# Running counts in PSUM, half a block at a time, and one PSUM bank for ranks and sums

## The chip, the cores and the metric

The kernel runs on one core of a Trainium2 chip. The metric is the device time of one execution in microseconds (us), lower is better. A core has a matrix engine (TensorE, PE in the profile; its weight loads are PEld), a vector engine (VectorE, DVE), a scalar engine (ScalarE, ACT), a general engine (GpSimd, POOL) and a queue engine that mostly issues transfers (SyncE, SP). Each works through its own instructions in order. They share an on-chip memory, SBUF, and an accumulator memory, PSUM, of eight banks with 512 fp32 values per partition each, into which TensorE writes.

## The reference

One layer of a graph network on 12,500 nodes with 64 features and 212,500 edges that are sorted by `dst`; `src` is in no order.

```python
h = jnp.maximum(_layernorm(x), 0.0)
edge_in = jnp.concatenate([h[src], h[dst], dist], axis=1)
e = silu(edge_in @ eW1 + eb1)
e = silu(e @ eW2 + eb2)
agg = jax.ops.segment_sum(e, src, num_segments=12500)
node_in = jnp.concatenate([h, agg], axis=1)
out = x + silu(node_in @ nW1 + nb1) @ nW2 + nb2
```

The sum over the edges goes by `src`, so edges that are far apart in the list are added to one node.

## The kernel before

**Buckets.** The nodes lie in 100 buckets of 125 (bucket = `src` mod 100). The edges are cut into 208 blocks of 1,024 (`BLK`), and the blocks into 11 chunks: the first has 8 blocks, the others 20 (the last of all is a little short). The work on a chunk has two halves.

- *Sending* (`count`, `send`): for each block, the share of every edge that comes from `dst` and the edge's weight is computed, and each edge's row is written to a place of its own in a DRAM table `q` of the chunk, in the part of its bucket.
- *Steps* (the `s_...` functions): the rows are fetched bucket by bucket, the share of `src` is added, both layers are applied and the rows of a bucket are summed per node. A step is four tiles of 128 rows. A batch is four buckets: one step in the first chunk, two in the others. There are 525 steps.

While the steps of chunk c run, chunk c+1 is sent. A fetch of a chunk's rows (`fetch`, issued on SP) can start when all scatters into its table are done.

**Where in its bucket does an edge go?** `count(s)` answers this for block s on DVE. `oh` (100 x 1,024, line 303) is 1 where an edge belongs to a bucket. A scan over the 1,024 columns (line 306) makes the running count `run` of each bucket: at each column it adds `oh` and a second input, `nil`, that is zero everywhere, and it starts from the last column of the block before (`carry`) or from -1. `nil` is one column, read with a stride of zero. The product of `run` and `oh` (line 314) is `own`, which keeps for each edge only the count of its own bucket. In `send(s)` eight matmuls against a column of fours (line 333) sum `own` over the buckets into `rank`, 128 x 8, and one DVE instruction (line 353) makes the row numbers `to` from it. Then POOL issues eight indirect transfers (line 362, "scatters"), each of 128 rows that are read at `qs` in SBUF and written to `q` at the rows in `to`.

**Where things lie.** All eight PSUM banks are taken: four for the rotating buffers tagged `mm`, two for `p2`, and two in the pool `sg`: one for `misc` (two rank buffers of 8 columns, used in turn by even and odd blocks, and the zero `nil`) and one for `seg`, the sums of a batch, 128 x 4 x 125. `oh`, `run` and `own` lie in SBUF (`own` twice).

**Order.** The order on PE, DVE, ACT and SP is the order of the program text; semaphores are put in from what each instruction reads and writes. A step's turn is the list at line 515: pt of the next step, the add of an earlier one's sums (`s_add`, which reads `seg` into `aggT`, once a batch), oneT, a hook, the bias, p2, one, a hook, `s_seg` (the matmuls into `seg`, line 497), a hook, lr, a hook. At the hooks the pieces of sending are put in at an even pace. A block has three pieces, and each goes one part on in `count(s + 1)` and then one part in `send(s)`:

1. pick and oh (lines 302, 303); the rank matmuls;
2. the load of edge weights and the scan; the matmuls qp with their copies on ACT, `to`, and the first four scatters;
3. the product own; the other four scatters.

`qs` has eight buffers of half a block and `to` four of a block, so POOL can be up to four blocks behind before ACT and DVE wait for it.

Of the kernel before, what the change touches and what calls it, by code (L numbers as in the profile page):

```python
# [38 lines left out]
P = 128  # L39
L = 125  # L40
# [19 lines left out]
def tile_gnn(ctx: ExitStack, tc: tile.TileContext, x, src, dst, ew, eW1, eb1, eW2, eb2, nW1, nb1, nW2, nb2, out):  # L60
# [178 lines left out]
    with ExitStack() as work:  # L239
# [5 lines left out]
                engines={mybir.EngineType.PE, mybir.EngineType.DVE, mybir.EngineType.Activation, mybir.EngineType.SP}  # L245
            )
        )
        misc = sgp.tile([P, 4 * TB], F32, name="misc")
        nc.vector.memset(misc[:, 2 * TB : 2 * TB + 1], 0.0)
        nil = misc[:NB, 2 * TB : 2 * TB + 1]  # L250
        oh = cnt.tile([NB, BLK], F16, name="oh")
        run = cnt.tile([NB, BLK], F32, name="run")
        carry = {}
        blk = {}
        nblocks = -(-E // BLK)
# [40 lines left out]
        def count(s):  # L296

            if s >= nblocks:
                return
            c = chunk_of[s]  # L300
            bc, bb, win, pick = blk[s]
            nc.vector.tensor_scalar(pick, bc, same, plus, op0=OP.is_equal, op1=OP.add)
            nc.vector.tensor_scalar(oh, bb[:NB, :], part[:NB, :], None, op0=OP.is_equal)
            yield
            weights(s)
            nc.vector.tensor_tensor_scan(  # L306
                run, oh, nil.to_broadcast([NB, BLK]), carry.get(c, -1.0), op0=OP.add, op1=OP.add
            )
            yield
            n = min(BLK, E - s * BLK)  # L310
            end = run[:, n - 1 : n]
            carry[c] = end
            own = wk.tile([NB, BLK], F16, name="own")
            nc.vector.tensor_tensor(own, run, oh, op=OP.mult)  # L314
            blk[s].append(own)
            if s + 1 == nblocks or chunk_of[s + 1] != c:
                u = wk.tile([NB, 1], F32, name="u")
                for limit, op in ((chunks[c][2] * P - 1, OP.is_gt), (chunks[c][3] - 1, OP.is_lt)):
                    nc.vector.tensor_scalar(u, end, float(limit), None, op0=op)
                    nc.vector.tensor_tensor(bad[:NB, 1:2], bad[:NB, 1:2], u, op=OP.add)  # L320
            yield

        def send(s):

            p, g = s // 2, s % 2
            c = chunk_of[s]
            _, _, cap, _, q = chunks[c]
            _, _, win, pick, run = blk.pop(s)
            n = min(BLK, E - s * BLK)
            nt = -(-n // P)  # L330
            rank = misc[:, (s % 2) * TB : (s % 2 + 1) * TB]
            for t in range(nt):
                nc.tensor.matmul(rank[:, t : t + 1], run[:, t * P : (t + 1) * P], fours[:NB, :], start=True, stop=True)  # L333
            yield

            qps = [mm.tile([P, G, H], F32, name="qp", tag="mm") for _ in range(2)]
            for t in range(G):
                for a in range(2):
                    half = slice(a * HB, a * HB + WL + 2)
                    if a * G + t < nt:  # L340
                        nc.tensor.matmul(  # L341
                            qps[a][:, t, :], pick[half, t * P : (t + 1) * P], win[half, :], start=True, stop=True
                        )
            halves = []
            for t0 in range(0, nt, G):
                qs = qsp.tile([P, G, W], F32, name="qs")
                m = min(G, nt - t0)
                nc.scalar.copy(qs[:, :m, :H], qps[t0 // G][:, :m, :])  # L348
                halves.append((t0, m, qs))
            for t0, m, qs in halves:  # L350
                if t0 == 0:
                    to = top.tile([P, TB], I32, name="to")
                    nc.vector.scalar_tensor_tensor(
                        to[:, :nt], rank[:, :nt], float(G * cap * P), bkE[:, g * TB : g * TB + nt, p], op0=OP.min, op1=OP.add
                    )
                at = g * TB + t0
                nc.scalar.copy(
                    qs[:, :m, H:], locE[:, at : at + m, p][:, :, None].to_broadcast([P, m, W - H])
                )
                for t in range(t0, t0 + m):  # L360
                    k = min(P, n - t * P)
                    i = nc.gpsimd.indirect_dma_start(  # L362
                        out=q[:],
                        out_offset=bass.IndirectOffsetOnAxis(ap=to[:k, t : t + 1], axis=0),
                        in_=qs[:k, t - t0, :],
                        in_offset=None,
                    )

                    tc.declare_no_dep(i.ins, group=f"rows{c}", reason="each edge has a row of its own")
                    tc.add_to_no_dep_group(f"rows{c}", i.ins)  # L370
                yield
# [25 lines left out]
        def fetch(i):  # L397
            if i >= len(batches):
                return
            c, B, n = batches[i]  # L400
            assert pending[c] == 0
            while B not in done_a:
                next(feed)
            q = chunks[c][-1]
            at = B * G * n * P
            qt = ld2.tile([P, G * most, W], F32, name="qt")
            nc.sync.dma_start(
                qt[:, : G * n, :].rearrange("p j w -> p (j w)"),
                q[at : at + G * n * P, :].rearrange("(p j) w -> p (j w)", p=P),
            )  # L410
            a3 = ld2.tile([P, G, 3, H], BF16, name="a3")
            nc.sync.dma_start(
                a3.rearrange("l b s f -> l b (s f)"), ta_buckets[:, B * G : B * G + G]
            )
            batch[c, B] = [qt, a3, None]
            if c == len(chunks) - 1:
                node_in[B] = nodes_in(B, ndp[0])

# [3 lines left out]
            return batch[c, B], [((g * G + t) % n * G + (g * G + t) // n, (g * G + t) // n) for t in range(G)]  # L422

        def s_lr(k):
            (qt, _, _), tiles = of(k)
            loc = qt.rearrange("p j w -> p (j w)").bitcast(BF16)
            lr = mm.tile([P, G, P], F32, name="lr", tag="mm")
            for t, (j, _) in enumerate(tiles):
                at = 2 * (j * W + H) + 1
                nc.tensor.matmul(lr[:L, t, :], loc[:, at : at + 1].to_broadcast([P, L]), identb, start=True, stop=True)  # L430
            st[k] = {"lr": lr}
# [5 lines left out]

        def s_pt(k):

            (qt, a3, _), tiles = of(k)  # L440
            oneT = st[k].pop("oneT")
            pt = mm.tile([P, G, P], F32, name="pt", tag="mm")
            for t, (j, _) in enumerate(tiles):
                nc.tensor.matmul(  # L444
                    pt[:, t, :], qt[:, j, :H], ident, is_transpose=True, start=t == 0, stop=False, skip_group_check=True
                )
            for b, same in itertools.groupby(range(G), lambda t: tiles[t][1]):
                same = list(same)
                cols = slice(same[0], same[-1] + 1)
                for i in range(3):  # L450
                    nc.tensor.matmul(  # L451
                        pt[:, cols, :], a3[:L, b, i, :], oneT[:, cols, :], start=False, stop=i == 2, skip_group_check=True
                    )
            e1 = wk.tile([P, G, P], F32, name="e1")
            nc.scalar.activation(e1, pt, AF.Silu)  # L455
            st[k]["e1"] = e1

        def s_one(k):
            (qt, _, _), tiles = of(k)
            c, B, n, g = steps[k]  # L460
            wide = [P, G // n, n, L]
            loc = qt[:, : G * n, H : H + 1].rearrange("p (j b) w -> p b j w", b=G)
            one = wk.tile([P, G, L], F32, name="one")
            nc.vector.tensor_tensor(  # L464
                one.rearrange("p (b j) l -> p b j l", j=n),
                nodes1[:, None, None, :].to_broadcast(wide),
                loc[:, tiles[0][1] : tiles[0][1] + G // n].to_broadcast(wide),
                op=OP.is_equal,
            )
            st[k]["one"] = one  # L470
            if g == n - 1:
                fetch(c * (NB // G) + B + NQ)
# [16 lines left out]

        def s_seg(k):  # L490
            c, B, n, g = steps[k]
            item, tiles = of(k)
            if g == 0:
                item[2] = sgp.tile([P, G, L], F32, name="seg")
            e2, one = st[k].pop("e2"), st[k].pop("one")
            for t, (j, b) in enumerate(tiles):
                nc.tensor.matmul(item[2][:, b, :], e2[:, t, :], one[:, t, :], start=j < G, stop=j >= G * (n - 1))  # L497

        def s_add(k):
            c, B, n, g = steps[k]  # L500
            if g < n - 1:
                return
            v = aggT[:, B * G : B * G + G, :]
            seg = batch.pop((c, B))[2]
            if c == 0:
                nc.vector.tensor_copy(v, seg)  # L506
            else:
# [425 lines left out]
```

## Time and profile before

| | |
|---|---|
| time, median of 3 runs | 2703.32 us (2700.62 to 2704.18) |
| the profiled execution | 2702.45 us |
| its span, first to last instruction | 2700.7 us |
| PE busy | 2188.2 us (81%) |
| DVE busy | 1874.6 us (69%) |
| POOL busy | 1818.5 us (67%) |
| ACT busy | 1251.1 us (46%) |
| mean TensorE clock granted | 0.907 |

The profile is of one execution. A group of instructions is named by its line in the kernel, its engine and operation, and what it writes and reads; behind it stand the count, the busy time, the mean duration of one in ns, and the idle time of the engine in front of it with what ended it. "Issue" is time in which the engine waited for nothing that the profile shows. The timeline lists instructions in order: start in us, duration in us, engine, line, operation; in brackets the idle time ahead of it. The windows view gives each engine's busy time and instruction count within stretches of the span. The chain of work that ended last puts 63% of the span on PE, 13% on DMA, 6% on issue, 5% on POOL and 2% on DVE.

### The profile page before, as it was taken

To read this page: it belongs to the slowest core of one execution; us is meant where nothing else is said; L and a number is where in the kernel's file an instruction comes from. 1 tells how busy PE (TensorE), PEld (TensorE's weight loads), DVE (VectorE), ACT (ScalarE), POOL (GpSimd) and SP (SyncE) were. 2 spreads that over 40 slices of the span, in tenths; PEclk is the share of its full clock that TensorE was granted. 3 is DMA by queue.
4 is the path that set the end of the run, shared out by engine and by line. 5 is a ranking of instruction groups with operands and counts; after the bars stand their busy time and mean duration, and the time that the engine had idled before them with its cause. 6 is when DMAs were issued, how large, how long until landed. Compare 5 with 4: busy or idle time off the path is not lost.

```text
span 2700.7 us, 59194 instructions
## 1 busy us (share of the span) xinstructions
PE 2188.2 (81%) x21814; PEld 2043.3 (76%) x21814; DVE 1874.6 (69%) x2634; ACT 1251.1 (46%) x2689; POOL 1818.5 (67%) x1728
## 2 busy tenths in 40 slices
PE   2436674898699599699879969959959987997997
PEld 1326574897699599599779869959958986996996
DVE  4736683796588488588768858848857885883443
ACT  2325551454355255355445535525535544553443
POOL 2546787777777777777777777777777777773000
PEclk9757786998899799799989989979989998998999
DMA  8668675876776777686787777767767755764441
GB/s 201 190 186 243 202 246 163 260 234 196 231 234 229 213 248 236 203 251 231 212 256 230 237 218 233 238 205 253 231 202 250 240 183 198 234 199 158 158 164 52
DMA packets 257969, 577.18 MB, mean 214 GB/s; under 512 B 51201, under 2 KB 110579, under 8 KB 257468
## 3 DMA queue, kind: packets, MB, share of 16 engines
q1 hardware_dynamic: 185096, 384.91, 44.3%
q0 software_dynamic: 54144, 123.04, 12.6%
q10 hardware_dynamic: 18434, 65.37, 10.5%
q8 instruction: 175, 2.87, 0.4%
q14 instruction: 120, 0.98, 0.1%
HBM read 361.44 MB, written 211.67 MB: 212 GB/s over the span
## 4 chain that ended last, share of the span: by engine, by line
PE 63%; DMA 13%; issue 6%; POOL 5%; DVE 2%; ACT 1%; SPq 0%; DVEq 0%; POOLq 0%; ACTq 0%
PE p L483 15%; PE seg L497 15%; PE pt L451 11%; DMA q<-qs,to 8%; PE pt L444 8%; PE qp L341 7%; POOL q L362 5%; PE lr L430 4%; DMA pick<-in_edge_weight_dram 3%; PE misc L333 1%; DMA bb<-rows 1%; PE z L216 1%; PE o L225 1%; DVE oneT L435 1%; PE z L219 1%
## 5 line engine op out<-in xcount | busy, mean ns | idle before, releaser
L362 POOL DMA_INDIRECT q<-qs,to x1661 | 1780.4, 1072 | 632.2 <-issue 445.6
L455 ACT ACTIVATE e<-pt 128x512 f32<-128x512 f32 x525 | 313.9, 598 | 778.0 <-PE pt L451 765.1
L483 PE MATMUL p<-w,e 128*128 128x128 f32 x4200 | 588.2, 284 | 2.2 <-ACT p L477 2.2
L497 PE MATMUL seg<-one,e 128*128 128x125 f32 x4200 | 576.8, 281 | 8.9 <-DVE aggT L506 5.7
L483 PEld LDWEIGHTS p<-w,e 128*128 128x128 f32 x4200 | 529.5, 198 | 27.5 <-issue 10.4
L497 PEld LDWEIGHTS seg<-one,e 128*128 128x128 f32 x4200 | 524.8, 196 | 11.2 <-ACT p L477 4.1
L435 DVE TENSOR_SCALAR oneT<-lr,part 125x512 bf16<-125x512 f32 x525 | 392.6, 748 | 197.5 <-PE lr L430 194.6
L306 DVE TENSOR_TENSOR_SCAN run<-oh,run,misc 100x1024 f32<-100x1024 f16 x197 | 461.1, 2341 | 1.0 <-PE misc L333 0.7
L451 PE MATMUL pt<-oneT,a 125*128 125x256 bf16 (+1 forms) x3300 | 444.6, 274 | 0.0
L341 PE MATMUL qp<-win,pick 50*128 50x128 f32 x3322 | 264.6, 300 | 205.0 <-DMA pick<-in_edge_weight_dram 119.9
L348 ACT COPY qs<-qp 128x512 f32<-128x512 f32 x416 | 224.7, 588 | 444.3 <-PE qp L341 312.0
L341 PEld LDWEIGHTS qp<-win,pick 50*128 50x128 f32 x3322 | 224.1, 202 | 237.8 <-issue 208.2
L444 PE MATMUL pt<-ident,qt 128*128 128x128 f32 x2100 | 332.8, 282 | 68.8 <-DVE oneT L435 68.8
L508 DVE TENSOR_TENSOR aggT<-aggT,seg 128x500 f32<-128x500 f32 x250 | 168.3, 673 | 315.7 <-PE seg L497 313.3
L464 DVE TENSOR_TENSOR one<-nodes,qt 128x500 f32<-128x500 f32 x525 | 353.4, 673 | 0.5 <-PE seg L497 0.5
L451 PEld LDWEIGHTS <-a 125*128 125x128 bf16 x3300 | 320.5, 100 | 34.5
L487 ACT ACTIVATE e<-p 128x512 f32<-128x512 f32 x525 | 314.6, 599 | 12.3 <-PE p L483 11.6
L477 ACT COPY p<-b2f 128x512 f32<-128x512 f32 x525 | 312.3, 595 | 0.1
L444 PEld LDWEIGHTS pt<-ident,qt 128*128 128x128 f32 x2100 | 228.4, 145 | 74.9 <-DVE oneT L435 72.9
L430 PE MATMUL lr<-identb,qt 128*125 128x128 bf16 x2100 | 215.1, 226 | 63.1 <-DMA qt<-q 63.0
L314 DVE TENSOR_TENSOR own<-run,oh 100x1024 f16<-100x1024 f32 x208 | 253.7, 1220 | 0.0
L430 PEld LDWEIGHTS <-qt 128*125 128x125 bf16 x2100 | 187.8, 140 | 75.6 <-DMA qt<-q 63.7
(122 smaller groups left out, 1094.5 us busy)
## 6 DMA issues: line engine op xcount, KB each, us to landing
qt<-q SPq DMA_DIRECT2D x250, 576.0 KB
a<-ta SPq DMA_DIRECT2D x275, 384.0 KB
q<-zeros ACTq DMA_DIRECT2D x30, 1638.0 KB
bb<-rows SPq DMA_DIRECT2D x208, 224.0 KB
bc<-rows SPq DMA_DIRECT2D x208, 128.0 KB
q<-qs,to POOLq DMA_INDIRECT x1661
win<-tb SPq DMA_DIRECT2D x416, 24.0 KB
ta<-parts SPq DMA_DIRECT2D x25, 384.0 KB
```

What stands on the lines that cost most here:

```text
L306: nc.vector.tensor_tensor_scan(run, oh, nil.to_broadcast([NB, BLK]), carry.get(c, -1.0), op0=OP.add, op1=OP.add)
L341: nc.tensor.matmul(qps[a][:, t, :], pick[half, t * P : (t + 1) * P], win[half, :], start=True, stop=True)
L362: i = nc.gpsimd.indirect_dma_start(out=q[:], out_offset=bass.IndirectOffsetOnAxis(ap=to[:k, t : t + 1], axis=0), in_=qs[:k, t - t0, :], in ...
L430: nc.tensor.matmul(lr[:L, t, :], loc[:, at : at + 1].to_broadcast([P, L]), identb, start=True, stop=True)
L435: nc.vector.tensor_scalar(oneT, st[k].pop("lr")[:L], part1[:L, :], None, op0=OP.is_equal)
L444: nc.tensor.matmul(pt[:, t, :], qt[:, j, :H], ident, is_transpose=True, start=t == 0, stop=False, skip_group_check=True)
L451: nc.tensor.matmul(pt[:, cols, :], a3[:L, b, i, :], oneT[:, cols, :], start=False, stop=i == 2, skip_group_check=True)
L455: nc.scalar.activation(e1, pt, AF.Silu)
L464: nc.vector.tensor_tensor(one.rearrange("p (b j) l -> p b j l", j=n), nodes1[:, None, None, :].to_broadcast(wide), loc[:, tiles[0][1] : ti ...
L483: nc.tensor.matmul(p2[:, t, :], e1[:, t, :], w2, start=False, stop=t == G - 1, skip_group_check=True)
L487: nc.scalar.activation(e2, p2, AF.Silu)
L497: nc.tensor.matmul(item[2][:, b, :], e2[:, t, :], one[:, t, :], start=j < G, stop=j >= G * (n - 1))
```

## The change

`run` becomes a PSUM tile of half a block (512 fp32 columns, one whole bank), in one buffer. The scan and the product are each done twice, for columns 0 to 511 and 512 to 1,023: scan, product, then the end of the piece, then scan and product of the second half. The second scan starts from the last column of the first; the carry from block to block is read from `run` too. So piece 2 has one half scan and one half product, and piece 3 the same; before, the scan was in piece 2 and the product in piece 3. `own` is allocated one piece earlier, ahead of the first scan.

To make room for `run` in PSUM, `misc` and `seg` become one tile in one bank: columns 0 to 499 are `seg`, columns 500 to 507 the one `rank` buffer. The sums of every batch lie in this tile for the whole run; before, a tile was allocated for each batch from a pool with one buffer. `nil` moves from PSUM to a column of its own in SBUF.

```diff
-        misc = sgp.tile([P, 4 * TB], F32, name="misc")
-        nc.vector.memset(misc[:, 2 * TB : 2 * TB + 1], 0.0)
-        nil = misc[:NB, 2 * TB : 2 * TB + 1]
+        misc = sgp.tile([P, G * L + TB], F32, name="misc")
+        seg = misc[:, : G * L].rearrange("p (b l) -> p b l", l=L)
+        rank = misc[:, G * L :]
+        run = sgp.tile([NB, HALF], F32, name="run")
         oh = cnt.tile([NB, BLK], F16, name="oh")
-        run = cnt.tile([NB, BLK], F32, name="run")
+        nil = cnt.tile([NB, 1], F32, name="nil")
+        nc.vector.memset(nil, 0.0)
...
             weights(s)
-            nc.vector.tensor_tensor_scan(
-                run, oh, nil.to_broadcast([NB, BLK]), carry.get(c, -1.0), op0=OP.add, op1=OP.add
-            )
-            yield
-            n = min(BLK, E - s * BLK)
-            end = run[:, n - 1 : n]
-            carry[c] = end
             own = wk.tile([NB, BLK], F16, name="own")
-            nc.vector.tensor_tensor(own, run, oh, op=OP.mult)
             blk[s].append(own)
+            for h in range(2):
+                half = slice(h * HALF, (h + 1) * HALF)
+                n = min(HALF, E - s * BLK - h * HALF)
+                if n <= 0:
+                    break
+                nc.vector.tensor_tensor_scan(
+                    run, oh[:, half], nil.to_broadcast([NB, HALF]), carry.get(c, -1.0), op0=OP.add, op1=OP.add
+                )
+                end = carry[c] = run[:, n - 1 : n]
+                nc.vector.tensor_tensor(own[:, half], run, oh[:, half], op=OP.mult)
+                if h == 0:
+                    yield
...
-            rank = misc[:, (s % 2) * TB : (s % 2 + 1) * TB]
...
-            if g == 0:
-                item[2] = sgp.tile([P, G, L], F32, name="seg")
             e2, one = st[k].pop("e2"), st[k].pop("one")
             for t, (j, b) in enumerate(tiles):
-                nc.tensor.matmul(item[2][:, b, :], e2[:, t, :], one[:, t, :], start=j < G, stop=j >= G * (n - 1))
+                nc.tensor.matmul(seg[:, b, :], e2[:, t, :], one[:, t, :], start=j < G, stop=j >= G * (n - 1))
...
             v = aggT[:, B * G : B * G + G, :]
-            seg = batch.pop((c, B))[2]
+            del batch[c, B]
```

More of the change, by code (lines that the diff above doesn't have):

```diff
@@ L414, in fetch @@
             )
-            batch[c, B] = [qt, a3, None]
+            batch[c, B] = [qt, a3]
             if c == len(chunks) - 1:
@@ L424, in s_lr @@
         def s_lr(k):
-            (qt, _, _), tiles = of(k)
+            (qt, _), tiles = of(k)
             loc = qt.rearrange("p j w -> p (j w)").bitcast(BF16)
@@ L438, in s_pt @@
         def s_pt(k):
-            (qt, a3, _), tiles = of(k)
+            (qt, a3), tiles = of(k)
             oneT = st[k].pop("oneT")
@@ L458, in s_one @@
         def s_one(k):
-            (qt, _, _), tiles = of(k)
+            (qt, _), tiles = of(k)
             c, B, n, g = steps[k]
@@ L491, in s_seg @@
             c, B, n, g = steps[k]
-            item, tiles = of(k)
-            if g == 0:
-                item[2] = sgp.tile([P, G, L], F32, name="seg")
+            _, tiles = of(k)
             e2, one = st[k].pop("e2"), st[k].pop("one")
             for t, (j, b) in enumerate(tiles):
-                nc.tensor.matmul(item[2][:, b, :], e2[:, t, :], one[:, t, :], start=j < G, stop=j >= G * (n - 1))
+                nc.tensor.matmul(seg[:, b, :], e2[:, t, :], one[:, t, :], start=j < G, stop=j >= G * (n - 1))
         def s_add(k):
```

## The prediction, made before the changed kernel was run

> **What bounds the kernel now.** I read the clock view first (0.907 on one core, nothing odd), then the windows by stage, cut at the ends of the chunks.
>
> ```profile
> core 0: us, PE busy (x) PEld busy (x) DVE busy (x) ACT busy (x) POOL busy (x), PEclk, DMA share, GB/s
> 240.00:460.00 220.00, 140.79 (x1380) 127.62 (x1380) 148.70 (x211) 103.96 (x238) 161.00 (x137) 0.77 0.63 203
> 680.00:901.00 221.00, 192.22 (x1979) 182.11 (x1980) 167.11 (x230) 107.09 (x230) 168.52 (x160) 0.94 0.73 230
> 1564.00:1785.00 221.00, 191.97 (x1982) 181.71 (x1981) 167.97 (x230) 107.67 (x230) 169.41 (x162) 0.93 0.73 231
> 2451.00:2701.00 250.00, 228.37 (x1951) 206.16 (x1951) 95.88 (x157) 103.30 (x204) 19.46 (x27) 0.96 0.42 139
> ```
>
> By busy time PE leads (192 of 221 us) and POOL stands at 169. But the line of the scatters says otherwise:
>
> ```profile
> L362 POOL DMA_INDIRECT q<-qs,to x1661: 889/967/3041, 67.7 to 2451.3; - x185
>   issue: 445.6, 1340
> ```
>
> A scatter takes 0.967 us, and the next one starts 0.30 us later although nothing is named that it waits for: one scatter each 1.27 us is POOL's own pace. A chunk has 20 blocks of 8 scatters. In chunk 3 (first scatter 691.9, last end 913.5, 221.6 us by the timeline) 160 x 1.27 = 203.2; scatters longer than 0.967 add 14.6, and gaps longer than 0.30 only 4.2. Chunks 3 to 9 are all so (219.7 to 221.3 us). So POOL sets the period of a chunk, and PE's 29 idle us are back-pressure: PE waits 19.15 us at 1564 for work whose loads stand in SP's queue behind a fetch that waits for the chunk's last scatter. After 2451 no scatter is left, and PE's 250 us of tail follow.
>
> The question is what stretches a scatter. I laid POOL's rows of the timeline against DVE's:
>
> ```profile
> 1564.12 2.34 DVE L306 TENSOR_TENSOR_SCAN run<-oh,run,misc 100x1024 f32<-100x1024 f16 x1
> 1564.62 0.97 POOL L362 DMA_INDIRECT q<-qs,to  x1 [0.30 <-issue]
> 1565.89 0.97 POOL L362 DMA_INDIRECT q<-qs,to  x1 [0.30 <-issue]
> 1566.37 0.14 DVE L353 SCALAR_TENSOR_TENSOR to<-misc,bkE 128x8 int32<-128x8 f32 x1
> 1566.43 0.67 DVE L464 TENSOR_TENSOR one<-nodes,qt 128x500 f32<-128x500 f32 x1
> 1567.01 1.22 DVE L314 TENSOR_TENSOR own<-run,oh 100x1024 f16<-100x1024 f32 x1
> 1567.16 1.92 POOL L362 DMA_INDIRECT q<-qs,to  x1 [0.30 <-issue]
> 1569.38 0.96 POOL L362 DMA_INDIRECT q<-qs,to  x1 [0.30 <-issue]
> ```
>
> Under the scan (inputs oh in SBUF and nil in PSUM) two scatters keep 0.97. The one that starts under own (run and oh, both in SBUF) takes 1.92 and ends 0.85 after own. Over the run, 210 scatters overlap a scan and no other DVE instruction: their mean excess is 0.001 us. 14 overlap own alone: 0.61. 44 overlap the add into aggT alone (one input in PSUM): 0.00. Instructions with a broadcast second input in SBUF stretch scatters too: beside L527 and L536 (mean and var) a scatter that starts 0.2 us in loses up to 0.67. Total excess over 0.967 is 175.6 us.
>
> [...]
>
> **The change part by part.**
>
> *Own from PSUM.* The product now has one SBUF input (oh). Of the 102.1 us of excess in chunks 3 to 9 (140 blocks, 0.73 each), 55 scatters end 0.84 behind own and carry 43.0 us, and 80 that are held by one and then by own carry 16.1; half of these to own makes 51 us, 0.36 a block. Shared out by overlap over the whole run, own has 81.4 us, 0.39 a block. I take 0.37 as what goes.
>
> *The scan with nil in SBUF.* This is the part that costs. The scan's two inputs are then oh and nil, both in SBUF, which it wasn't before, and it comes twice a block. No run shows such a scan. Bounds: nothing if the scan doesn't hold POOL; about 0.95 us a half (what a scatter lost at the worst phase of own) if each half does its worst, 1.9 a block. I take the rule that own's rows give: a scatter that starts under the instruction ends 0.84 after it, one started up to 0.5 before it ends 0.30 before its end. Applied to a 1.28 us instruction at the 140 places where scans start now, it gives 0.77 each, because starts cluster 0.15 and 0.42 us ahead of a scatter. At even phase it gives 0.68, times 0.73 (for own the rule gives 0.44 at its true places against 0.61 at even phase) 0.49. A held POOL also shifts its own phase, so I take the mean, 0.63, for the first half. The second lies where own lay: 0.39 x 1.28/1.22 = 0.40. Together 1.03 a block. Net 1.03 - 0.37 = +0.66 us a block, x 200 blocks of chunks 1 to 10 = +132 us. Chunk 0 (8 blocks) has 44 us of other gaps between its scatters; half price, +3.
>
> *DVE's time.* Rows: 500 elements 673 ns (L464), 1,024 elements 1,220 (L314), so 1.044 ns an element and 151 fixed; a PSUM input costs no more (L508, 500 elements, also 673). A half product is 686, two 1,371: +151. The scan with a constant start is 2,278, with a carried one 2,341: 2.08 ns an element, 151 fixed, 63 for the carry. A half is 1,277, two 2,554: +213. Writing PSUM instead of SBUF is not in the trace; I take it equal, within 0.1 us a half. In all +364 ns a block, 76 us of DVE time. It is hidden: DVE idles 53 us a chunk and gets 7 more. Without that cover it would be the 76 us.
>
> *Split of the pieces.* DVE's longest stretch ahead of oneT falls from 2.34 to 1.28 + 0.69 = 1.97, the next grows from 1.22 to 1.97. PE's 68.8 us of waits for oneT are mostly back-pressure (DVE stands 7.63 us at `to` for a scatter's DMA at 1554), so nothing.
>
> *Seg and rank in one bank, one rank buffer.* New waits: seg's matmuls for the `to` in front of them, rank's matmuls for the add into aggT, `to` for the seg matmuls in front. Behind a waiting seg stand lr, pt and all of PE; `to` is queued behind a half scan and a half product, at worst 1.97 us, x 20 = 39 us a chunk if nothing covers it. Cover: p2 or qp of the same turn (1.1 us each on PE) and PE's 29 idle us a chunk. DVE has run ahead to wait for seg 134 times (313 us), so `to` mostly comes early. Between 0 and 39 a chunk; I take 0, as PE's loss up to 29 only eats its wait for POOL. The memory that run frees in SBUF is used by nothing. Loads and scatters keep their number and order.
>
> *Sum.* 2702.45 (the profiled execution, 1.75 above its span, 0.9 under the median) + 132 + 3 = 2837 us.
>
> **Rivals.**
> - *The scan with a stride-0 nil does not hold POOL* (faster). Price: only own's 0.37 goes, x 200 = 74 us, so 2628; PE's 192 us still fit in 214 a chunk. For it: nil is one column, and no scan with two SBUF inputs was seen. Against it: mean and var are broadcast too and hold. It decides as soon as a half scan holds POOL for under 0.18 us.
> - *The product still holds POOL through its one SBUF input* (it doesn't do what it says). Two products of 0.69; one (0.67) lost 0.1 to 0.45 by phase when a scatter started under it. 0.15 each, +0.30 a block: 2837 + 60 = 2897. Against it: L508 reads one operand of each kind and cost nothing.
> - *The bank's waits bind PE.* If all 39 us a chunk show, 10 over PE's slack: +100, hidden in a POOL that is itself 13 us a chunk slower; on top of a faster POOL it would undo the gain, 2700.
> - *Half holding*: 0.3 a half, +0.23 a block, 2750.
>
> **How the numbers follow.** Forecast 0.66, with its own range 2770 (net 0.34 a block) to 2900 (0.98); product also holds 0.09; between, by the last two rivals, 0.07; scan doesn't hold 0.18. From 2680 to 2930 lie 0.65 of the first, 0.08 of the second and the 0.07: 0.80. This kernel's three times lie within 0.13%, so 0.2% (5.4 us) is what can be told from no change. Faster 0.20 (the 0.18 and a little of the 0.07), same 0.02, slower 0.78.
>
> **What would show it.** In the changed trace: a chunk's period near 234 us with 160 scatters; scatters beside a lone half scan with a mean excess of 0.4 or more, ending 0.84 behind it; those beside a lone half product at 0; L362's mean about 1,150 ns against 1,072; half scans near 1,277 ns and half products near 686; seg's waits for `to` small. Wrong if scatters keep 0.97 under half scans, if chunks fall to 213 us, or if PE's idle time is named by the bank's waits while POOL starves.

## The result, and the profile after

The changed kernel takes 2717.64 us (median of 9 runs, 2712.54 to 2721.56), the kernel before 2703.27 us (9 runs). The ratio is 1.0054, 95% interval 1.0041 to 1.0067: slower by 14 us, where the forecast had 134. The span of its profiled execution is 2719.8 us, 19.1 more than before.

The windows view of the changed kernel, with the windows of the prediction (busy us and count for PE, PEld, DVE, ACT and POOL, then clock, DMA share, GB/s; the last window reaches to the end):

```profile
680.00:901.00 221.00, 192.77 (x1973) 182.00 (x1974) 170.07 (x263) 106.92 (x229) 170.03 (x160) 0.93 0.70 223
1564.00:1785.00 221.00, 193.12 (x1980) 182.02 (x1980) 174.19 (x267) 106.86 (x228) 169.71 (x159) 0.93 0.73 230
2451.00:2720.00 269.00, 233.69 (x2011) 211.14 (x2009) 98.60 (x162) 106.38 (x210) 35.01 (x42) 0.94 0.40 133
```

The stages look alike; POOL still handles its 160 scatters a chunk, and its last one ends 20 us later (2472.1 against 2452.2), so the tail begins 20 us later and is as long as before. By the timeline chunks 3 to 9 take 223.5 us on average from the first scatter's start to the last one's end (before 220.9; forecast 234). The groups of instructions that the prediction priced:

```profile
L367 POOL DMA_INDIRECT q<-qs,to x1661 | 1795.4, 1081 | 637.0 <-issue 450.7
...
L315 DVE TENSOR_TENSOR_SCAN run<-oh,run,nil 100x512 f32<-100x512 f16 x405 | 523.0, 1291 | 0.1
...
L319 DVE TENSOR_TENSOR own<-run,oh 100x512 f16<-100x512 f32 x416 | 287.7, 691 | 14.2
```

A half scan takes 1,291 ns and a half product 691, as priced (1,277 and 686). But the mean scatter went from 1,072 to 1,081 ns only, not to 1,150. Does a half scan hold POOL at all (does a scatter that meets it have to wait for its end)? The timeline of the changed kernel, DVE and POOL rows side by side, two places:

```profile
843.60 0.67 DVE L469 TENSOR_TENSOR one<-nodes,qt 128x500 f32<-128x500 f32 x1
844.18 1.29 DVE L315 TENSOR_TENSOR_SCAN run<-oh,run,nil 100x512 f32<-100x512 f16 x1
844.54 1.70 POOL L367 DMA_INDIRECT q<-qs,to  x1 [0.30 <-issue]
845.51 0.69 DVE L319 TENSOR_TENSOR own<-run,oh 100x512 f16<-100x512 f32 x1
...
1603.05 0.67 DVE L469 TENSOR_TENSOR one<-nodes,qt 128x500 f32<-128x500 f32 x1
1603.37 1.18 POOL L367 DMA_INDIRECT q<-qs,to  x1 [0.30 <-issue]
1603.63 1.29 DVE L315 TENSOR_TENSOR_SCAN run<-oh,run,nil 100x512 f32<-100x512 f16 x1
1604.86 0.97 POOL L367 DMA_INDIRECT q<-qs,to  x1 [0.31 <-issue]
1604.96 0.69 DVE L319 TENSOR_TENSOR own<-run,oh 100x512 f16<-100x512 f32 x1
```

It does. The scatter that starts 0.36 us into the half scan takes 1.70 us and ends 0.77 after the scan (846.24 against 845.47). The scatter at 1603.37 starts ahead of the half scan and under `one`. It takes 1.18 us and ends 0.83 after `one` (1604.55 against 1603.72): that is the hold of `one`, and the half scan adds nothing to it. The next starts 0.06 us before the scan's end and under the product, and takes 0.97.

The whole trace says the same. Of the scatters that start 0.02 to 0.5 us ahead of a half scan, the 149 with `one` in front of the scan end 0.84 after `one` (median), and the 32 with oneT there, which holds nothing (the 22 that overlap oneT alone lose 0.00 us), keep 0.97. A scatter that starts under a half scan loses the less the later it starts: 0.73 us at 0.36 us in, 0.45 at 0.65 us in, and nothing (0.01 at most) in the last 0.1 us. So the direction of each hold is as forecast, and the price of a half scan ranges from nothing to 0.95 us with its place in POOL's cycle.

To add this up I gave each scatter's excess over 0.967 us to the DVE instruction that runs 0.12 us after the scatter's start (a scatter needs 0.84 us after a product that held it and 0.967 by itself, so what can be held lies about 0.13 us behind its start), then to the one that follows without a break, and what is left to the last holder that it overlaps. In us a block, chunks 3 to 9:

| kernel | median us | a chunk | all excess | own | scans | one | pick, oh |
|---|---|---|---|---|---|---|---|
| before | 2703.3 | 220.9 | 0.73 | 0.31 | 0.00 | 0.26 | 0.16 |
| changed | 2717.6 | 223.5 | 0.89 | 0.00 | 0.61 | 0.18 | 0.09 |
| nil away, run as second input (e1) | 2635.2 | 214.1 | 0.38 | 0.00 | 0.00 | 0.31 | 0.07 |
| before, nil in SBUF (e2) | 2977.0 | 251.5 | 2.38 | 0.50 | 1.42 | 0.29 | 0.15 |
| before, shared bank alone (e3) | 2725.3 | 223.6 | 0.85 | 0.47 | 0.00 | 0.20 | 0.18 |
| before, halves in SBUF alone (e4) | 2675.2 | 218.7 | 0.60 | 0.16 | 0.00 | 0.33 | 0.10 |

The half products from PSUM hold nothing: in the whole trace 134 scatters meet one, and the largest excess among them is 0.01 us.

The two half scans of a block differ. The first costs 0.49 us on average and the second 0.13 (140 of each). A scatter starts 0.05 to 0.8 us into 105 of the first and into only 33 of the second; 98 of the second start within 0.3 us behind a scatter's start, which is too late to hold it (the 32 above kept 0.97).

### The profile page after: what moved, and what is told of

It is laid out like the page before. It is cut to its first block, busy times and chain, and to the rows that moved or that the text cites. A ratio compares the mean times of both kernels' runs of the same rounds, so it can differ in the third digit from the quotient of the medians.

```text
span 2719.8 us, 59549 instructions
## 1 busy us (share of the span) xinstructions
PE 2193.4 (81%) x21814; PEld 2042.9 (75%) x21814; DVE 1957.2 (72%) x3050; ACT 1249.8 (46%) x2689; POOL 1833.7 (67%) x1728
## 3 DMA queue, kind: packets, MB, share of 16 engines
q14 instruction: 123, 1.01, 0.1%
## 4 chain that ended last, share of the span: by engine, by line
PE 49%; DMA 12%; POOL 5%; issue 5%; DVE 2%; ACT 1%; SPq 0%; DVEq 0%; POOLq 0%; ACTq 0%
PE p L488 12%; PE misc L500 12%; PE pt L456 8%; DMA q<-qs,to 7%; PE pt L449 6%; PE qp L346 5%; POOL q L367 5%; PE lr L435 3%; DMA pick<-in_edge_weight_dram 3%; DMA bc<-rows 1%; PE z L216 1%; PE o L225 1%; PE misc L338 1%; DVE oneT L440 1%; DMA q<-zeros 1%
## 5 line engine op out<-in xcount | busy, mean ns | idle before, releaser
L367 POOL DMA_INDIRECT q<-qs,to x1661 | 1795.4, 1081 | 637.0 <-issue 450.7
L500 PE MATMUL misc<-one,e 128*128 128x125 f32 x4200 | 580.6, 282 | 27.9 <-DVE to L358 17.5
L500 PEld LDWEIGHTS misc<-one,e 128*128 128x128 f32 x4200 | 525.2, 196 | 37.2 <-issue 17.2
L315 DVE TENSOR_TENSOR_SCAN run<-oh,run,nil 100x512 f32<-100x512 f16 x405 | 523.0, 1291 | 0.1
L346 PE MATMUL qp<-win,pick 50*128 50x128 f32 x3322 | 266.9, 302 | 214.1 <-DMA pick<-in_edge_weight_dram 121.1
L511 DVE TENSOR_TENSOR aggT<-aggT,misc 128x500 f32<-128x500 f32 x250 | 167.7, 671 | 287.5 <-PE misc L500 276.2
L319 DVE TENSOR_TENSOR own<-run,oh 100x512 f16<-100x512 f32 x416 | 287.7, 691 | 14.2
```

Source lines behind the costliest of these rows:

```text
L315: nc.vector.tensor_tensor_scan(run, oh[:, half], nil.to_broadcast([NB, HALF]), carry.get(c, -1.0), op0=OP.add, op1=OP.add)
L346: nc.tensor.matmul(qps[a][:, t, :], pick[half, t * P : (t + 1) * P], win[half, :], start=True, stop=True)
L367: i = nc.gpsimd.indirect_dma_start(out=q[:], out_offset=bass.IndirectOffsetOnAxis(ap=to[:k, t : t + 1], axis=0), in_=qs[:k, t - t0, :], in ...
L500: nc.tensor.matmul(seg[:, b, :], e2[:, t, :], one[:, t, :], start=j < G, stop=j >= G * (n - 1))
```

## The experiments

### Which second input the scan has (e1_max, e2_nil)

In the changed kernel, e1_max takes `run` itself, in PSUM, as the scan's second input and combines by max; `nil` goes. Within a chunk a count never falls, so an old count is never above the new one, and at the start of a chunk `run` is set to -1:

```diff
...
-                nc.vector.tensor_tensor_scan(
-                    run, oh[:, half], nil.to_broadcast([NB, HALF]), carry.get(c, -1.0), op0=OP.add, op1=OP.add
-                )
+                if c not in carry:
+                    nc.vector.memset(run, -1.0)
+                nc.vector.tensor_tensor_scan(run, oh[:, half], run, carry.get(c, -1.0), op0=OP.add, op1=OP.max)
```

> The changed kernel, but the scan's second input is run itself, in PSUM, combined by max instead of nil by add (old counts are never above new ones; run is set to -1 at the start of a chunk). Neither scan nor product then has two SBUF inputs. Theory A (POOL sets the pace, and what changed is how long DVE holds it): excess per block in the even chunks falls from 0.89 us to 0.2 to 0.35 (pick, oh and one are left), a chunk from 223.5 to 210 to 213 us, time 2590 to 2635. Theory B (the lost time comes from waits on the bank that seg and rank share, or from DVE's longer work): those stay, time 2705 or more. Theory C (POOL has slack): time within 10 us of 2718 although the scatters get shorter.

Measured: 2635.18 us, ratio 0.9743 (0.9728 to 0.9758). The groups view of this run, the scatters and the two halves' instructions:

```profile
L365 POOL DMA_INDIRECT q<-qs,to x1661 | 1699.3, 1023 | 647.8 <-issue 452.4 <-ACT qs L360 80.2 <-DMA q<-qs,to 48.2
...
L315 DVE TENSOR_TENSOR_SCAN run<-oh,run 100x512 f32<-100x512 f16 x416 | 534.3, 1284 | 0.5
L317 DVE TENSOR_TENSOR own<-run,oh 100x512 f16<-100x512 f32 x416 | 287.7, 692 | 14.4
```

DVE's instructions are as many and as long as in the changed kernel (1,284 against 1,291 ns), the bank is still shared, and 82 us are gone. They are nil's. Theories B and C fall. Theory A holds, its ranges missed by a little: 0.38 us of excess a block against 0.2 to 0.35, 214.1 us a chunk against 210 to 213. This version is faster than both kernels, by 68 us against before.

The other way round, e2_nil is the kernel before with one edit:

```diff
-        nc.vector.memset(misc[:, 2 * TB : 2 * TB + 1], 0.0)
-        nil = misc[:NB, 2 * TB : 2 * TB + 1]
+        nil = cnt.tile([NB, 1], F32, name="nil")
+        nc.vector.memset(nil, 0.0)
```

> The kernel before with one edit: nil in SBUF instead of PSUM. The whole scan of 2.34 us then has two SBUF inputs. Theory A: each scan holds POOL, 1.1 to 1.8 us a block by the rule (starts spread evenly at the low end, as they lie before at the high end), so 2920 to 3060 us. Theory C: less than half of that shows in the time, below 2810.

Measured: 2976.97 us, ratio 1.1003 (1.0985 to 1.102). From the timeline of this run:

```profile
1498.55 0.67 DVE L464 TENSOR_TENSOR one<-nodes,qt 128x500 f32<-128x500 f32 x1
1498.73 1.33 POOL L362 DMA_INDIRECT q<-qs,to  x1 [0.30 <-issue]
1499.13 2.35 DVE L306 TENSOR_TENSOR_SCAN run<-oh,run,nil 100x1024 f32<-100x1024 f16 x1
1500.36 1.89 POOL L362 DMA_INDIRECT q<-qs,to  x1 [0.30 <-issue]
1502.56 0.96 POOL L362 DMA_INDIRECT q<-qs,to  x1 [0.31 <-issue]
```

The scan has its old length (2,345 against 2,341 ns), and the scatter that starts under it ends 0.77 after it. A scan longer than POOL's cycle can hardly miss a scatter: 1.42 us each. All excess rose by 1.65 us a block and a chunk by 30.6 us. Theory A's ranges hold, and a stride-0 column in SBUF counts as a second input (1.42 us a scan, 0.00 with the column in PSUM). The scatter at 1498.73, under `one`, ends 0.84 after `one` and 1.42 before the end of this long scan.

### The shared bank alone (e3_bank), and one rank buffer (e8_onerank)

The kernel before with `seg` and one `rank` buffer in one tile, as in the changed kernel; `nil` gets the freed bank, `run` and `own` stay whole and in SBUF:

```diff
-        misc = sgp.tile([P, 4 * TB], F32, name="misc")
-        nc.vector.memset(misc[:, 2 * TB : 2 * TB + 1], 0.0)
-        nil = misc[:NB, 2 * TB : 2 * TB + 1]
+        misc = sgp.tile([P, G * L + TB], F32, name="misc")
+        seg = misc[:, : G * L].rearrange("p (b l) -> p b l", l=L)
+        rank = misc[:, G * L :]
+        nil = sgp.tile([NB, 1], F32, name="nil")
+        nc.vector.memset(nil, 0.0)
...
```

> The kernel before with only seg and the (single) rank buffer in one tile of one bank; nil has the freed bank, run and own as before. Theory A: PE's new waits for `to` fall into its wait for POOL, time 2703 plus or minus 4. Theory B: at least 8 us slower, 2711 or more.

Measured: 2725.26 us, ratio 1.0075 (1.0061 to 1.0089). Theory A's number is wrong, and the prediction's with it; Theory B's holds: seg and one rank buffer in one bank cost 22 us. PE's new waits for `to` are small, though:

```profile
PE misc L496 <- DVE to L354: 28.3, 43, 7.4
```

That is 28 us in 43 waits, of 208 possible. POOL is as tight as before: gaps beyond its 0.30 us stay at 4 to 5 us a chunk. What grew is what the same product own, with the same inputs and length (1,219 ns), takes from POOL: 0.47 instead of 0.31 us a block, while `one` takes 0.06 less. A scatter starts under 94 of the 140 products there, under 57 before: own has come to a dearer place in POOL's cycle. That is seen; which of the new waits moves it was not tried. One part of the edit, the lost second rank buffer, was tried alone:

```diff
-            rank = misc[:, (s % 2) * TB : (s % 2 + 1) * TB]
+            rank = misc[:, :TB]
```

> The kernel before with one rank buffer instead of two, in its bank as before; seg keeps its own bank. Tells whether the 22 us of the shared bank alone come from the lost second rank buffer. If from the bank that seg shares: 2703 plus or minus 4. If from the single buffer: 2715 or more.

This and all later runs fell on chips on which the kernel before takes 3362 to 3464 us; there POOL's gaps beyond its 0.30 us come to 64 to 86 us a chunk (108 to 145 in e5_b2b and e9_max2, 3 to 5 before), so POOL does not set the pace. Their times can't be set beside the numbers above, only beside those of the kernel before on the same chip. e8_onerank: ratio 0.9998 (0.9972 to 1.0024).

> The kernel before with one rank buffer instead of two, seg in its own bank, again where POOL sets the pace. If the 22 us of the shared bank come from the bank: 2703 plus or minus 4. If from the lost second buffer: 2715 or more.

On another such chip: 1.0062 (1.0025 to 1.01). Neither settles it for a kernel that POOL paces.

### The halves alone (e4_half)

The kernel before with the loop over two halves of the changed kernel, `run` of 512 columns in SBUF, `nil` in PSUM and the banks as before.

> The kernel before with scan and product in two halves, run half a block in SBUF, nil in PSUM, banks as before. DVE gets some 76 us of work more; the products of 0.69 us each have two SBUF inputs. Theory A: two products cost POOL about as much as own did or somewhat less (0.2 to 0.4 us a block against 0.36), time 2670 to 2710. Theory B (DVE's added work costs): 2715 or more.

Measured: 2675.19 us, ratio 0.9898 (0.9882 to 0.9914), 28 us faster with more DVE work: its scans and products come to 817.2 us (515.8 + 13.3 + 288.1) against 739.9 before. Theory B falls: DVE's added work has cover. Two products of 693 ns take 0.16 us a block from POOL where one of 1,220 took 0.31, a little less than Theory A had. A scatter that starts under a short holder should have less of it left to wait for, as it ends 0.84 after a product that held it (before); the place was not held fixed, so how much of the gain is the length and how much the place isn't known. Chained up, the parts are: halves 2703 to 2675, run in PSUM with the shared bank and no nil (e1) to 2635, nil in SBUF back up to 2718.

### What sets the price of a half scan (e5_b2b, e6_gap, e7_gapend)

Three changes of place. e5_b2b puts both halves into piece 2:

```diff
                 nc.vector.tensor_tensor(own[:, half], run, oh[:, half], op=OP.mult)
-                if h == 0:
-                    yield
+            yield
```

e6_gap puts `nc.vector.memset(gap, 0.0)` on a scratch tile of 100 x 256 (272 ns) ahead of each half scan, e7_gapend the same behind each half product. Behind a memset the half scan's record is shorter, 1,170 ns against 1,291.

> The changed kernel with scan, product, scan, product all in piece 2, nothing between the halves and nothing in piece 3. The number, length and inputs of the instructions are the same, only the place of the second half scan in POOL's cycle is another. Theory P (what a half scan costs is set by where in POOL's 1.27 us cycle it starts): the scatter held by the first half ends 0.77 after it, the next one starts 0.30 later, 0.4 to 0.5 us into the second half scan, and loses about 0.6 us each time instead of 0.31: 0.2 to 0.3 us a block more, 2750 to 2780 us. Theory F (each half scan has a fixed price): within 8 us of 2718.

> The changed kernel with a memset of 100 x 256 fp32 on a scratch tile ahead of each half scan: it reads nothing from SBUF, adds some 0.33 us of DVE work and parts the half scan from the product `one` ahead of it. Theory P: [...] half scans rise from 0.31 to 0.4 to 0.55 us each, 0.2 to 0.5 us a block, 2755 to 2815 us. Theory F: within 8 us of 2718, as DVE has the time.

> As the run before, with the same memset behind each half product instead of ahead of the half scan. DVE's added work is the same, the half scan stays directly behind `one`. Theory P: half scans keep 0.25 to 0.4 us each, and the time is nearer to 2718 than that of the other place by 25 us or more. Theory F, or DVE's added work as the cause: both places give the same time.

All of them fell on the slower chips. e6_gap and e7_gapend were run again on three more chips, e5_b2b on two, with expectations that repeat these; e5_b2b's second adds a theory:

> The back-to-back halves again (scan, product, scan, product in piece 2, piece 3 empty), as in the first try the kernel before took 3398 us, its scatters apart by gaps of 5 us and more, so that POOL did not set the pace. With the kernel before near 2703: Theory P (the price of a half scan is set by where in POOL's 1.27 us cycle it starts): the second half starts 0.4 to 0.5 us into a scatter and costs about 0.6 us, 2750 to 2780 us. Theory F (fixed price): within 8 us of 2718. The first try adds a third way, theory D: 3.9 us of DVE work in one stretch hold up PE, which shows as PE's wait for oneT and as gaps between scatters.

> The memset (0.27 us) ahead of each half scan again, on a chip where POOL sets the pace. Theory P: half scans rise from 0.31 to 0.4 us or more each, time 2740 to 2815 us. Theory F: within 8 us of 2718.

> The memset (0.27 us) behind each half product again. Theory P: half scans directly behind `one` keep their price, and the time is 25 us or more nearer to 2718 than with the memset ahead. Otherwise both places give the same time.

> The memset (0.27 us) ahead of each half scan. To be read where the kernel before takes about 2703 us. Theory P (the price of a half scan hangs on where in POOL's 1.27 us cycle it starts, and directly behind `one` that is a cheap place): half scans rise from 0.31 to 0.4 us or more each, time 2740 to 2815 us. Theory F (a fixed price): within 8 us of 2718.

> The memset (0.27 us) behind each half product. Theory P: half scans directly behind `one` keep their price, and the time is 25 us or more nearer to 2718 than with the memset ahead. Otherwise both places give the same time.

> Scan, product, scan, product in piece 2, piece 3 empty. Theory P: the second half scan starts 0.4 to 0.5 us into a scatter and costs about 0.6 us, 2750 to 2780 us. Theory F: within 8 us of 2718. Theory D (from the tries where POOL did not set the pace): `to` stands behind 3.9 us of DVE work and seg's matmuls wait for it, which shows as PE's wait for `to` (225 us there) and as gaps between scatters, time above 2780.

> The memset (0.27 us) ahead of each half scan, hoped to fall where the kernel before takes about 2703 us. Theory P (the price of a half scan hangs on where in POOL's 1.27 us cycle it starts, and directly behind `one` that is a cheap place): half scans rise from 0.31 to 0.4 us or more each, time 2740 to 2815 us. Theory F (a fixed price): within 8 us of 2718.

> The memset (0.27 us) behind each half product. Theory P: half scans directly behind `one` keep their price, and the time is 25 us or more nearer to 2718 than with the memset ahead. Otherwise both places give the same time.

| kernel | ratio to the kernel before, 95% interval, chip by chip |
|---|---|
| e5_b2b, two stretches in one | 1.110 (1.101 to 1.119), 1.125 (1.119 to 1.131), 1.138 (1.133 to 1.144) |
| e6_gap, memset ahead | 1.011 (1.008 to 1.014), 1.012 (1.009 to 1.015), 1.013 (1.009 to 1.016), 1.010 (1.006 to 1.014) |
| e7_gapend, memset behind | 1.008 (1.005 to 1.011), 1.012 (1.007 to 1.016), 1.010 (1.006 to 1.014), 1.007 (1.004 to 1.010) |

The test of theory P against F by time thus failed: in none of these runs did POOL set the pace, and the changed kernel itself was not run on these chips. What a half scan costs can still be added up from the timelines, in us each, chunks 3 to 9:

| kernel | first half, behind `one` | first half, behind oneT | second half, behind `one` | mean |
|---|---|---|---|---|
| changed | 0.54 | 0.43 | 0.13 | 0.31 |
| e6_gap, four runs | 0.24 to 0.28 | 0.09 to 0.20 | 0.47 to 0.57 | 0.34 to 0.41 |
| e7_gapend, four runs | 0.19 to 0.38 | 0.04 to 0.16 | 0.41 to 0.47 | 0.29 to 0.36 |

In e6_gap the memset stands between. P's 0.4 is reached in one of its four runs, just. A fixed price doesn't fit either: the second halves cost 0.13 in one kernel and three to four times that in the others, and the first halves go the other way. "Behind `one` is cheap" is no rule: `one` stands ahead of the dearest and of the cheapest half scans of the changed kernel. That a half scan behind the memset would hold again a scatter that `one` had held was the author's estimate for e6_gap. The timelines show no such scatter: one that `one` held ends 0.84 after `one`, whatever follows.

e5_b2b is theory D. In the waits of its second run PE's seg matmuls wait for `to`, which stands behind 3.9 us of DVE work:

```profile
PE misc L499 <- DVE to L357: 225.5, 83, 12.4
PE misc L499 <- ACT e L459: 112.5, 34, 5.6
```

That is the shared bank's wait which the prediction bounded at 39 us a chunk, and it shows that the wait is real when the stretch ahead of `to` is long. How much of the 11 to 14% it is was not taken apart. The second half scans, for which P had 0.6 us, cost 0.02 to 0.07 there, with POOL's gaps at their largest.

### The faster version once more (e9_max2)

> The changed kernel with run as the scan's second input and max, once more. Where the kernel before takes about 2703 us: ratio 0.97 to 0.98 as at first. Where it takes 3390 us or more, POOL has gaps of some 80 us a chunk of its own and holding it less should buy little. Theory A (holds cost only where POOL sets the pace): ratio 0.99 to 1.005 there. If holds cost whatever sets the pace: 0.98 or less (68 us of 3400).

Measured where the kernel before takes 3434 us: ratio 1.0675 (1.0605 to 1.0746). Neither case of the expectation: it isn't merely without gain, it is slower there. Its page and that of e8_onerank2 (ratio 1.006), from like chips, begin so:

```profile
PE 2816.7 (76%) x21814; PEld 2490.4 (68%) x21814; DVE 1969.0 (53%) x3060; ACT 1262.1 (34%) x2689; POOL 1716.9 (47%) x1728
```

```profile
PE 2676.5 (79%) x21814; PEld 2361.9 (69%) x21814; DVE 1886.0 (55%) x2634; ACT 1251.5 (37%) x2689; POOL 1847.9 (54%) x1728
```

POOL's busy time fell as it should. PE is busy for 2,817 us with the same 21,814 matmuls for which this same version took 2,169 in e1_max. The granted clock is lower there too, 0.807 here and 0.841 in e8_onerank2 against 0.922 in e1_max and 0.907 before. Whether that is the cause, and why this version is slower still, stays open. The 68 us hold where POOL sets the pace, and no further.

## Why the prediction was right in kind and wrong in size

- *POOL sets the pace*: right. Excess per block times 200 blocks gives the time of three runs: e1 (0.38 - 0.73) x 200 = -70 us, measured -68; e3 +24, measured +22; e4 -26, measured -28. For e2 it gives +330 against +274 and for the changed kernel +32 against +14. In both, chunk 1, in which other work is fed in too, came out shorter than the excess says (+8.9 us against +33 in e2, -5.6 against +3 in the changed kernel), and POOL's gaps beyond 0.30 us shrank, from 4.0 us a chunk to 1.5 and 3.4. The changed kernel's profiled execution is also the slowest of its nine: by the spans the difference is 19 us.
- *Own goes, -0.37 a block*: right, 0.31 in size. The 0.06 between comes from a misreading. The prediction gave own half of the excess of 80 scatters "that are held by one and then by own". A scatter that starts under `one` ends 0.84 after `one` in front of own, in front of a half scan and in front of a scan that holds nothing (17 cases before), so all of it is `one`'s, and own's are the 43.0 us alone. The prediction's rule that a scatter "started up to 0.5 before it ends 0.30 before its end" is the same misreading: 0.30 before the end of own, 0.37 before that of a half scan and 1.42 before that of e2's whole scan are all 0.92 us behind its start. The product from PSUM holds nothing, so "the product still holds POOL" falls.
- *The scan with nil in SBUF holds POOL*: right, and with it the faster rival falls; 2635 us in e1 is what that rival (2628) would have been.
- *"Together 1.03 a block. Net 1.03 - 0.37 = +0.66 us a block"*: this is the step that failed, in the size of its first term. The half scans took 0.61 us a block. That is 0.42 x 200 = 84 us of the 120 that are missing. The larger part is the second half, forecast at 0.40 because it "lies where own lay" and measured at 0.13: it lies there in the order of the program, but not in POOL's cycle. Only 33 of 140 have a scatter start 0.05 to 0.8 us into them, and 98 come just behind a scatter's start. The first half, forecast at 0.63, took 0.49. Of the two averages behind 0.63, the 0.77 from the present places was the worse: it took over places from a kernel in which scans hold nothing. Before, 62 of 140 scans had a scatter start 0.05 to 0.35 us into them, the dear place; in the changed kernel 22 of 280 half scans do. The other average, 0.49 from even spacing, is what came, in part by luck: its rule counts scatters that start ahead of the scan, which the scan does not hold (about 0.1 of its 0.68, an estimate: 0.5 x 0.5 / 2 over a cycle of 1.27), and the places aren't even. The pattern repeats, as with the 1.70 us scatters at 844.54 and at 881.93, each 0.36 us into a half scan. A term left out is the neighbours: `one`, pick and oh gave back 0.15 us a block (0.42 to 0.27), 30 us; the prediction changed nothing on them. Own's 0.06 goes the other way, 12 us. Why the places come out as they do is argued, not shown: when POOL sets the pace, DVE waits for POOL (`to` for a scatter's DMA, 69.2 us in 19 waits in the changed kernel) as well as holding it, so each hold moves the next.
- *The rival "half holding"*, 0.3 a half, had the price of a half scan; its 2750 lacks what the neighbours gave back.
- *DVE's time hidden*: right. DVE's busy time rose by 82.6 us (1874.6 to 1957.2; forecast 76), and e4 is faster in spite of it. *Splitting, nothing*: right for DVE's work, as far as e4 shows; its gain is own's price by another road.
- *Seg and rank in one bank, 0*: wrong by itself, +22 us in e3, and by another road than the one bounded: not PE's idle time but own's place. In the changed kernel own doesn't hold, so how much of it is left there isn't known. That seg's waits for `to` would be small there is right, 17.5 us in 12 waits:

```profile
PE misc L500 <- DVE to L358: 17.5, 12, 5.4
```

The other two new waits that it named are in this trace as well: rank's matmuls (L338) for the reading of seg into aggT, 9.0 us in 3 waits, and `to` for the seg matmuls, 1.2 us in 2.

## What to carry to other kernels

When GpSimd's transfers set the pace, as one each 1.27 us did here, count which VectorE instructions have two SBUF inputs, a stride-0 constant included (own 0.31 us a block before, e2's scan 1.42), and price them together: moving one operand to PSUM (own from 0.31 to 0.00) is undone if the operand's neighbour leaves PSUM for it (the scans from 0.00 to 0.61). Two tensors are not all: oh, which reads one tensor and one value per partition, stretched scatters too (the 36 that overlap it alone before lost 0.19 us on average). The price of a hold here was between nothing and what was left of the holder when a scatter met it (0.73 us at 844.54, with 0.93 of the half scan left). Places taken over from the old kernel missed it here by a factor of 1.6 (0.77 for 0.49) and of three (0.40 for 0.13), so the range should say so. A running count that can't fall needs no zero operand: its own old values in PSUM, combined by max, do (e1, where the scans took 0.00 us a block and the time fell 82 us below the changed kernel's).

## What the hardware did that was not expected

- A scatter ends 0.77 us after a scan that held it (188 in the changed kernel), against 0.84 after a product (82 before, medians). One that starts under `one` ends 0.84 after `one`, whatever instruction comes next. One moment of a scatter that can be held, about 0.13 us after its start (an estimate, 0.967 less 0.84), explains all of this; nothing here shows a second.
- A half scan into PSUM takes 1,291 ns, into SBUF with nil in PSUM 1,274 (e4), into PSUM with run as second input 1,284 (e1): at most 17 ns for the places of the output and the second input.
- Shorter holders cost less than their share: two products of 693 ns 0.16 us, one of 1,220 ns 0.31.
- The kernel before took 2701 to 2712 us in its first 18 runs and 3362 to 3464 us on the chips of all later ones. One version of the kernel was busy on PE for 2,169 us on the one (granted clock 0.922) and 2,817 on the other (0.807) with the same matmuls, and an edit worth -2.6% on the one was +6.7% on the other.
